# One table of step times for all engines in a stack of linear-attention layers, with eight shared PSUM banks

## The chip, the cores and the metric

The kernel runs on one core of a Trainium2 chip. The metric is device time in microseconds (us), from launch to finish, over repeated runs of the same program; less is better. A core has a matrix engine (TensorE, PE in the profile), which multiplies into PSUM, an on-chip memory of eight banks, and three engines that work on vectors: VectorE (DVE), ScalarE (ACT) and GpSimd (POOL). GpSimd has no part in reading PSUM in this kernel. DMA queues, most of them issued by the SyncE queue (SP), move data between device memory and the on-chip memory SBUF. Each engine works its own queue of instructions in order, and engines wait for each other by semaphores.

## What is computed

Two sequences of 2048 tokens with 256 features each, all in float32, go through two stacks. The first stack has three layers of causal linear attention (16 heads, 16 features each) with an MLP of 1024 hidden units:

```python
def favor(x, omega):
    xs = x * dh ** (-0.25)
    u = jnp.einsum('bshd,dm->bshm', xs, omega)
    h = 0.5 * jnp.sum(xs * xs, axis=-1, keepdims=True)
    return jnp.concatenate([jnp.exp(u - h), jnp.exp(-u - h)], axis=-1) * m ** (-0.5)

def step(carry, qkv):                      # causal linear attention, token by token
    Sst = Sst + ki[..., :, None] * vi[..., None, :]
    zst = zst + ki
    num = jnp.einsum('bhm,bhmd->bhd', qi, Sst)
    den = jnp.einsum('bhm,bhm->bh', qi, zst) + ATTN_EPS
    return ((Sst, zst), num / den[..., None])

for l in range(L):
    q, k, v = (out @ Wq[l] + bq[l]), (out @ Wk[l] + bk[l]), (out @ Wv[l] + bv[l])   # by heads
    a = causal_linear_attention(favor(q, omega[l]), favor(k, omega[l]), v) @ Wo[l] + bo[l]
    h = layer_norm(out + a, ln1_g[l], ln1_b[l])
    y = jax.nn.relu(h @ W1[l] + bf1[l]) @ W2[l] + bf2[l]
    out = layer_norm(h + y, ln2_g[l], ln2_b[l])
```

Its input is a normalized x, scaled and shifted by a conditioning vector; its output goes, gated, back onto x. The second stack has two layers of softmax attention in windows and a gated MLP. The change doesn't touch it.

## The kernel before

**Tiling.** The linear stack works on blocks of 256 tokens (TA): 2 sequences x 8 = 16 blocks, each through three layers, 48 layer passes in all. Between passes over the same sequence and layer, a running state (`state`, `zsum`) is carried, so a block's pass needs the state that the block before it left. A layer is `favor_layer` (L471). It has these steps, by the names of the tiles in the profile:

- projections `pq` (twice, queries and keys, L484) and `pv` (L500); VectorE adds the bias into `xs` (L495), ScalarE squares it (L496), VectorE fills `vp` (L511);
- features: `pu` (L525), eight matmuls that use 64 of the 128 columns of TensorE's array each (`tile_position=(0, 64 * hf)`), and their exponentials `ft` (L535); `qe` (L541), running sums `z` (L547, then GpSimd L556, L557), the transposed keys `tk` (L561) and `ktm` (L563);
- scores: `sc` (L572) for each half of 128 tokens, eight matmuls that use 32 of the 128 rows each, into four banks; VectorE masks each bank into `att` (L578);
- sums for the state: `su` (L592), `sum` (L600), `sth` and `st` on GpSimd (L612, L665); denominators `den` (L620) and `rb` (L622, L623);
- weighted values: `nd`, from the states with the whole array (L631), from the masked scores with 32 columns each (L644), then `aT` (L667);
- output projection `po` (L674), sum `s` (L682), the norm (`normed`: L422 to L430), its transpose `ntp` (L440), `h1` (L444);
- MLP: eight times `pf` (L696), `fr` (L704) and `acc` (L707), then the sum (L719), the norm, and the transpose into the next layer's `h`.

`scaled` (L453, L454, and L451 where a third operand is added) makes the residual on GpSimd. After the last layer a block's result is scaled onto its x, stored, normalized, transposed and stored again (`favor_block`, L763).

**Banks.** PSUM's eight banks are split in three: three for `mm_tile`, four shared by `sc` and `pf`, one for `acc`.

**Order.** `favor_layer` and `favor_block` are generators. Between two `yield`s lies a piece of TensorE work; the `yield` gives the planner `planned` (L91) a cost, a time until the next piece is due, a lock ("attention" or "mlp") and a piece of another block that must be done first. With at most four blocks in flight, the planner picks the piece that is due first. The order that results is fixed for TensorE alone (`manual_schedule(engines={PE})`, L793). The instructions of VectorE, ScalarE, GpSimd and the DMA queues are placed by the framework's own scheduler. It also picks the bank or buffer, out of those with the same tag, that a new tile gets.

The second stack already takes its steps from a table, `WHEN` (L124), on all four compute engines, with one pool of eight banks.

Of the kernel before, what the change touches and what calls it, by code (L numbers as in the profile page):

```python
# [39 lines left out]
def block_kernel(ctx: ExitStack, tc: tile.TileContext, t: dict, out: bass.AP):  # L40
# [48 lines left out]
    done = set()  # L89

    def planned(jobs, at_once):  # L91

        jobs, live, held, now, count = iter(jobs), [], {}, 0.0, 0
        while True:
            while len(live) < at_once:
                g = next(jobs, None)
                if g is None:  # L100
                    break
                live.append([now, count, g, None, None])
                count += 1
            if not live:
                return
            e = min(
                e[:2] + [e] for e in live
                if held.get(e[3], e) is e and (e[4] is None or e[4] in done)
            )[2]
            if e[3]:  # L110
                held[e[3]] = e
            step = next(e[2], None)
            keep = step[2] if step and len(step) > 2 else None
            for k in [k for k, o in held.items() if o is e and k != keep]:
                del held[k]
            if step is None:
                live.remove(e)
                continue
            now = max(now, e[0]) + step[0]
            e[0] = now + step[1]  # L120
            e[3:] = list(step[2:]) + [None] * (4 - len(step))
# [99 lines left out]
    with ExitStack() as c1:  # L221
        psum = c1.enter_context(tc.tile_pool(name="psA", bufs=1, space=PSUM))
        rp = c1.enter_context(tc.tile_pool(name="rA", bufs=2))
# [13 lines left out]

        def mm_tile(name):
            return psum.tile([P, TB], F32, tag="mm", name=name, bufs=3)
# [68 lines left out]
        def spread(lo, hi):  # L308
            n = (hi - lo) * KT
            tp = mm_tile("rowtp")[:n, :P]  # L310
            nc.tensor.transpose(tp, cols[:, lo:hi, :].rearrange("p a k -> p (a k)"), ident)
            turned_ = turned_cols.pop()[:n]
            nc.scalar.copy(turned_, tp)
            nc.gpsimd.dma_start(rows_out[lo * KT : hi * KT], turned_)
            nc.gpsimd.dma_start(
                brow[:, lo:hi, :].rearrange("p a d -> p (a d)"),
                rows_out[lo * KT : hi * KT].rearrange("a c -> (a c)").partition_broadcast(P),
            )
# [41 lines left out]
        def first_norm(normed, turned):  # L360

            with tc.manual_schedule(
# [6 lines left out]
                pm = mm_tile("pm")  # L369
# [22 lines left out]
        def rest_of_setup():  # L392
            yield 0.0, 8.0, "mlp"
            pm = psum.tile([P, NCA * D], F32, tag="acc", name="pm2", bufs=1)
            for i in range(2, 6):
                condition(i, i + 1, pm)
                yield 1.7, 0.0, "mlp"
            conditioned(2, 6, pm)
            for l in range(1, LA):
                omega_rows(l)  # L400
            for i in (2, 5):
# [10 lines left out]
            yield 0.0, 2.5  # L412
            spread(R_GE, NROW)
            load_weights(2, "Wq", "Wk", "Wv", "Wo", "W1", "W2")
            yield 0.2, 0.0

        def normed(src, dn=None):

            mv = work.tile([P, NCA, 2], F32, tag="mv", name="mv")
            for c in range(NCA):  # L420
                bs = work.tile([P, 6], F32, tag="bs", name="bs")
                nc.vector.bn_stats(bs, src[:, c, :])  # L422
                nc.vector.bn_aggr(mv[:, c, :], bs)
            rs = work.tile([P, NCA], F32, tag="rs", name="rs")
            nc.scalar.activation(rs, mv[:, :, 1], AF.Ln, bias=eps_t)
            nc.scalar.activation(rs, rs, AF.Exp, scale=-0.5)
            if dn is None:
                dn = work.tile([P, NCA, D], F32, tag="dn", name="dn", bufs=3)
            for c in range(NCA):
                nc.vector.tensor_scalar(  # L430
                    dn[:, c, :], src[:, c, :], mv[:, c, 0:1], rs[:, c : c + 1], ALU.subtract, ALU.mult
                )
            return dn

        def turned(dn, dst, gain, bias):

            tp = mm_tile("ntp").rearrange("p (k c) -> p k c", k=KT)
            for kt in range(KT):
                for c in range(NCA):
                    nc.tensor.transpose(  # L440
                        tp[:, kt, c * P : (c + 1) * P], dn[:, c, kt * P : (kt + 1) * P], ident
                    )
            for kt in range(KT):
                nc.scalar.activation(dst[:, kt, :], tp[:, kt, :], AF.Identity, bias=bias(kt), scale=gain(kt))  # L444

# [25 lines left out]
        def favor_layer(b, n, l, h, hres):  # L471
            va = V_A + l * VA_N

            def v(name, i=0):
                return vec[:, va + VA[name] + i : va + VA[name] + i + 1]

            xs = {}
            for wn, bn in (("Wq", "bq"), ("Wk", "bk")):  # L480
                pq = mm_tile("pq").rearrange("p (g c) -> p g c", g=KT)
                for g in range(KT):
                    for kt in range(KT):
                        nc.tensor.matmul(  # L484
                            pq[:, g, :],
                            W[wn, l][:, kt, g * P : (g + 1) * P],
                            h[:, kt, :],
# [3 lines left out]
                xs[wn] = fp.tile([P, 2, KT, TA], F32, tag="xs", name="xs", bufs=2)  # L491
                bias = vec[:, va + VA[bn] : va + VA[bn] + KT].unsqueeze(2).to_broadcast([P, KT, TA])
                for hf in range(2):
                    own, other = slice(64 * hf, 64 * hf + 64), slice(64 - 64 * hf, 128 - 64 * hf)
                    nc.vector.tensor_tensor(xs[wn][own, hf], pq[own], bias[own], ALU.add)  # L495
                    nc.scalar.activation(xs[wn][other, hf], xs[wn][own, hf], AF.Square)  # L496
            pv = mm_tile("pv").rearrange("p (c d) -> p c d", c=NCA)
            for c in range(NCA):
                for kt in range(KT):
                    nc.tensor.matmul(  # L500
                        pv[:, c, :],
                        h[:, kt, c * P : (c + 1) * P],
                        W["Wv", l][:, kt, :],
                        start=(kt == 0),
                        stop=(kt == KT - 1),
                    )

            vp = vpads[turn[0] % len(vpads)]
            turn[0] += 1
            for c in range(NCA):  # L510
                nc.vector.tensor_tensor(  # L511
                    vp[:, c, :, 0::3, :],
                    pv[:, c, :].rearrange("p (i q d) -> p i q d", q=2, d=16),
# [3 lines left out]
            yield 5.2, 0.6, "attention"  # L517
            if callable(hres):
                hres = hres()
            feat = []  # L520
            for wn in ("Wq", "Wk"):
                pu = mm_tile("pu").rearrange("p (g c) -> p g c", g=KT)
                for g in range(KT):
                    for hf in range(2):
                        nc.tensor.matmul(  # L525
                            pu[64 * hf : 64 * hf + 64, g, :],
                            omt[:, l, hf].rearrange("p h s m -> p (h s m)"),
                            xs[wn][:, hf, g, :],
                            start=True,
                            stop=True,  # L530
                            skip_group_check=True,
                            tile_position=(0, 64 * hf),
                        )
                ft = fp.tile([P, KT, TA], F32, tag=f"f{wn}", name="ft", bufs=1)
                nc.scalar.activation(ft, pu, AF.Exp)  # L535
                feat.append(ft)
            qf, kf = feat

            qe = sp.tile([P, KT, 2, TA], F32, tag="qe", name="qe", bufs=1)
            for q in range(2):  # L540
                nc.vector.tensor_scalar(qe[:, :, q, :], qf, par[:, q : q + 1], None, ALU.mult)  # L541
            yield 2.0, 1.0, "attention"

            z = fp.tile([P, KT, TA], F32, tag="z", name="z", bufs=1)
            zb = zsum.get((b, l))
            for g in range(KT):
                nc.vector.tensor_tensor_scan(  # L547
                    z[:, g, :],
                    kf[:, g, :],
# [5 lines left out]
            zsum[b, l] = sp.tile([P, KT], F32, tag=f"z{b}{l}", name="zl")  # L555
            nc.gpsimd.tensor_copy(zsum[b, l].unsqueeze(2), z[:, :, TA - 1 : TA])  # L556
            nc.gpsimd.tensor_tensor(z, qf, z, ALU.mult)  # L557
            tk = mm_tile("tk").rearrange("p (c g f) -> p c g f", c=NCA, g=KT)
            for c in range(NCA):
                for g in range(KT):  # L560
                    nc.tensor.transpose(tk[:, c, g, :], kf[:, g, c * P : (c + 1) * P], ident)  # L561
            ktm = fp.tile([P, NCA, KT, P], F32, tag="ktm", name="ktm", bufs=1)
            nc.scalar.copy(ktm, tk)  # L563

            def scores(c):

                cs = slice(c * P, (c + 1) * P)
                scs = [psum.tile([P, KT, 2, P], F32, tag="sc", name="sc", bufs=4) for _ in range(4)]
                for g in range(KT):
                    for i in range(4):  # L570
                        rs_ = slice(32 * i, 32 * i + 32)
                        nc.tensor.matmul(  # L572
                            scs[i][:, g], kf[rs_, g, cs], qe[rs_, g, :, cs], start=True, stop=True
                        )
                out_ = []
                for i in range(4):
# [948 lines left out]
```

## Time and profile before

| | us |
|---|---|
| median of 3 runs | 2959.73 |
| lowest, highest | 2957.91, 2963.54 |
| profiled execution | 2958.75 |
| its span, first to last instruction | 2957.0 |
| first projection of the linear stack (pq) starts | 11.63 |
| last MLP of the linear stack (acc) ends | 1560.36 |
| first projection of the second stack (pqkv) starts | 1561.36 |

| stretch, us | TensorE busy | VectorE busy | ScalarE busy | GpSimd busy |
|---|---|---|---|---|
| 0 to 60 | 48.92 | 38.61 | 20.06 | 28.57 |
| 120 to 1000 | 875.33 | 499.36 | 346.91 | 250.07 |
| 1000 to 1500 | 493.80 | 283.73 | 195.50 | 149.26 |
| 1700 to 1800 | 100.00 | 76.52 | 70.42 | 67.91 |

The page has one row for a group of instructions: line, engine, operation, the tiles written and read, their shapes, the count; then busy time in all and the mean of one in ns; then the idle time of the engine just before such instructions and what ended most of it. A row in order of time has the start, the duration (both in us), the engine, the line and the count. A TensorE row reads `128*32 128x256` where 128 rows and 32 columns of the array are used and 256 columns of data stream through. Each float32 matmul of the kernel is two records, a transpose is one.

### The profile page before, as it was taken

The page shows a single profiled execution, that of the slowest core. Times are in us where ns is not written, and L with a number is a line of the kernel's source. Part 1 is how long each engine was busy: PE and PEld are TensorE (multiplying, and loading weights), DVE is VectorE, ACT ScalarE, POOL GpSimd, SP SyncE. Part 2 cuts the span into 40 slices and gives each one's busy share as a digit, 9 for nine tenths or more (in the row PEclk, how much of TensorE's full clock was granted, in tenths as well). Part 3 has the DMA queues.
Part 4 walks back from the last instruction along what each step waited for, and adds up shares of the span by engine and source line. Part 5 has one row for each costly group of instructions (what it writes and reads, how often), then busy time and mean ns, then how long its engine had stood idle before and what let it go on. Part 6 is the DMA issues. An engine that isn't in the chain of part 4 may idle for free.

```text
span 2957.0 us, 49152 instructions
## 1 busy us (share of the span) xinstructions
PE 2904.0 (98%) x19323; PEld 2125.8 (72%) x19323; DVE 1688.3 (57%) x4186; ACT 1339.7 (45%) x3263; POOL 1068.9 (36%) x937
## 2 busy tenths in 40 slices
PE   8999999999999999999998999999999999999999
PEld 6888888888888888788875777775444777776444
DVE  6555556555655555655546777773224777774222
ACT  3343344343433343434335766675114667666211
POOL 4222233222332223322235666662002666663000
PEclk9999999999999999999999999999999999999999
DMA  6000010000100001001011000001000000000011
GB/s 218 1 1 1 5 39 15 1 1 1 41 18 1 1 1 37 19 1 44 16 54 39 5 20 1 1 1 58 0 0 10 1 20 1 1 1 8 29 43 36
DMA packets 38791, 58.96 MB, mean 20 GB/s; under 512 B 4702, under 2 KB 29856, under 8 KB 37920
## 3 DMA queue, kind: packets, MB, share of 16 engines
q1 hardware_dynamic: 36608, 51.33, 5.4%
q8 instruction: 153, 2.51, 0.4%
q0 software_dynamic: 1136, 3.44, 0.3%
q10 hardware_dynamic: 816, 1.05, 0.1%
q14 instruction: 78, 0.64, 0.1%
HBM read 43.73 MB, written 12.08 MB: 19 GB/s over the span
## 4 chain that ended last, share of the span: by engine, by line
PE 88%; DVE 5%; ACT 3%; POOL 2%; issue 1%; DMA 0%; SPq 0%; DVEq 0%; ACTq 0%; POOLq 0%
PE pf L696 11%; PE acc L707 11%; PE pqkv L914 9%; PE pg L1259 6%; PE pq L484 5%; PE acc L1297 5%; PE pa L1259 5%; PE av L1103 3%; PE ptp L1077 3%; PE sim L1010 3%; PE po L1122 3%; PE nd L644 3%; PE sc L572 3%; PE pu L525 3%; PE pv L500 3%; PE po L674 3%
## 5 line engine op out<-in xcount | busy, mean ns | idle before, releaser
L696 PE MATMUL pf<-h,wa 128*128 128x256 f32 x1536 | 402.5, 385 | 0.6 <-DVE att L578 0.3
L707 PE MATMUL acc<-wb,fr 128*128 128x256 f32 x1536 | 397.4, 382 | 4.8 <-ACT fr L704 4.4
L704 ACT ACTIVATE fr<-pf,vec 128x256 f32<-128x256 f32 x384 | 180.6, 471 | 429.4 <-PE pf L696 428.6
L914 PE MATMUL pqkv<-wqkv,s 128*128 128x512 f32 x768 | 352.0, 594 | 1.0 <-PE acc L707 1.0
L578 DVE TENSOR_TENSOR att<-sc,cst 128x512 f32<-128x512 f32 x384 | 238.1, 681 | 157.5 <-PE sc L572 157.5
L707 PEld LDWEIGHTS acc<-wb,fr 128*128 128x128 f32 x1536 | 288.5, 190 | 51.4 <-ACT fr L704 7.7
L696 PEld LDWEIGHTS pf<-h,wa 128*128 128x128 f32 x1536 | 277.3, 191 | 55.5 <-issue 19.8
L453 POOL TENSOR_TENSOR res<-dn,brow 128x512 f32<-128x512 f32 x110 | 143.4, 1304 | 457.6 <-DVE dn L430 442.0
L1065 POOL TENSOR_TENSOR pm<-pm,sum 128x1024 f32<-128x1024 f32 (+1 forms) x128 | 235.7, 1842 | 181.9 <-DVE sum L1060 181.9
L1050 ACT ACTIVATE pm<-pm,mx 128x256 f32<-128x256 f32 (+1 forms) x512 | 249.6, 488 | 60.3 <-DVE mx L1042 60.1
L956 POOL TENSOR_TENSOR rot<-raw,rsn_wo 128x512 f32<-128x512 f32 x128 | 160.7, 1276 | 197.9 <-ACT raw L937 194.7
L914 PEld LDWEIGHTS pqkv<-wqkv,s 128*128 128x128 f32 x768 | 136.3, 191 | 126.4 <-issue 124.0
L1268 DVE SCALAR_TENSOR_TENSOR ge<-pa,vec,ge 128x512 f32<-128x512 f32 x80 | 60.0, 751 | 280.7 <-PE pa L1259 229.4
L1267 ACT ACTIVATE ge<-pg,vec 128x512 f32<-128x512 f32 x96 | 65.8, 685 | 314.6 <-PE pg L1259 314.6
L496 ACT ACTIVATE xs<-xs 64x512 f32<-64x512 f32 x192 | 120.6, 628 | 152.9 <-DVE xs L495 143.6
L1259 PE MATMUL pg<-s,w 128*128 128x512 f32 (+1 forms) x384 | 182.2, 597 | 0.0
L484 PE MATMUL pq<-h,wa 128*128 128x256 f32 x768 | 177.4, 385 | 0.7 <-ACT h L444 0.7
L495 DVE TENSOR_TENSOR xs<-pq,vec 64x512 f32<-64x512 f32 x192 | 132.2, 688 | 75.8 <-PE pq L484 72.0
L1297 PE MATMUL acc<-ge,w 128*128 128x512 f32 (+1 forms) x384 | 168.8, 600 | 0.0
L484 PEld LDWEIGHTS pq<-h,wa 128*128 128x128 f32 x768 | 147.4, 193 | 22.9 <-issue 1.4
L1122 PEld LDWEIGHTS po<-oT,rsn_wo 128*128 128x128 f32 x1024 | 125.5, 194 | 38.1 <-issue 26.8
L978 POOL TENSOR_TENSOR qk<-qk,rot 128x1024 f32<-128x1024 f32 x64 | 151.3, 2365 | 0.5
(177 smaller groups left out, 5371.6 us busy)
## 6 DMA issues: line engine op xcount, KB each, us to landing
xin<-in_x_dram SPq DMA_DIRECT2D x30, 256.0 KB, 3.0
xl<-x SPq DMA_DIRECT2D x8, 512.0 KB, 4.3
out_dram<-res SPq DMA_DIRECT2D x8, 512.0 KB, 3.1
w<-in_w_dram SPq DMA_DIRECT2D x6, 640.0 KB, 4.1
x<-res SPq DMA_DIRECT2D x14, 256.0 KB, 2.1
h<-hm SPq DMA_DIRECT2D x14, 256.0 KB, 2.4
wa<-in_W_dram SPq DMA_DIRECT2D x3, 1024.0 KB, 11.1
wb<-in_W_dram SPq DMA_DIRECT2D x3, 1024.0 KB, 12.0
```

The costliest lines, as they stand in the source:

```text
L484: nc.tensor.matmul(pq[:, g, :], W[wn, l][:, kt, g * P : (g + 1) * P], h[:, kt, :], start=(kt == 0), stop=(kt == KT - 1),)
L578: nc.vector.tensor_tensor(am, scs[i].rearrange("p g q c -> p (g q) c"), caus.unsqueeze(1).to_broadcast([P, 2 * KT, P]), ALU.mult,)
L696: nc.tensor.matmul(pf, W["W1", l][:, kt, f * P : (f + 1) * P], h1[:, kt, :], start=(kt == 0), stop=(kt == KT - 1),)
L704: nc.scalar.activation(fr[f], pf, AF.Relu, bias=v("bf1", f))
L707: nc.tensor.matmul(acc[:, c, :], fr[f - 1][:, c * P : (c + 1) * P], W["W2", l][:, f - 1, :], start=(f == 1 and c == 0), stop=(f == NF), sk ...
L914: nc.tensor.matmul(pq, s[:, kt * TB + c * P : kt * TB + (c + 1) * P], wqkv[:, kt, i * INNER : (i + 1) * INNER], start=(kt == 0), stop=(kt ...
L956: nc.gpsimd.tensor_tensor(rot[:, :, :, lo : lo + 32], got["raw"][:, :, :, hi : hi + 32], rsn[:, ti, :, lo : lo + 32].unsqueeze(2).to_broad ...
L1050: nc.scalar.activation(pm[:, hd, :], pm[:, hd, :], AF.Exp, bias=of("mx", hg)[:, hd : hd + 1], accum_out=of("sum", hg)[:, hd : hd + 1],)
L1065: nc.gpsimd.tensor_tensor(pm, pm, of("sum", hg).unsqueeze(2).to_broadcast([P, 4, kw]), ALU.mult)
L1122: nc.tensor.matmul(po[:, m, :], wo[:, k, m * P : (m + 1) * P], got["oT"][:, k, :], start=(k == 0), stop=(k == INNER // P - 1),)
L1259: nc.tensor.matmul(pt[:m, :], w1[:, kt, off : off + m], hb[:, kt * TB : (kt + 1) * TB], start=(kt == 0), stop=(kt == KT - 1),)
L1297: nc.tensor.matmul(acc[m], w2[rs_, f, m * P : (m + 1) * P], g[rs_, :], start=(f == 0), stop=(f == NFH - 1),)
```

## The change

The generators and the planner go. `favor_layer(k)` now returns the steps of layer pass k as named functions, and a table gives each name a time, in units of one layer pass. Step `name` of pass k is placed at k + WHEN_A[name]; all steps are sorted by that, and TensorE, VectorE, ScalarE and GpSimd take them in this order (from 49.6 on only TensorE's is fixed). Passes go by fours: layer 0 of four blocks, layer 1 of the same four, layer 2, then the next four blocks. So passes k and k + 4 belong to the same block, or, after a third layer, to the block that leaves and the one that enters.

Besides this: all tiles in PSUM come from one pool of eight banks (`bank`); the features `pu` (step U) are cut into 16 matmuls of 32 columns instead of 8 of 64; the weighted values take both states first and then the scores of both halves; there are 10 instead of 8 buffers of masked scores, 2 instead of 1 of query features, 2 instead of 3 of `h1`; the loads for the second stack are issued two passes before the last.

```diff
-    def planned(jobs, at_once):
...
+    WHEN_A = {
+        "load": -1.9, "x0": -1.316, "x1": -1.297, "xr": -1.273, "xd0": -1.252, "xd1": -1.237,
+        "xput": -1.236, "T2": -1.23, "resB": -1.218, "h": -1.189, "Pq": -1.174, "Pk": -1.118, "xq0":
+        -1.085, "xq1": -1.063, "sq0": -1.057, "sq1": -1.035, "xk0": -1.029, "xk1": -1.007, "sk0":
+        -1.001, "sk1": -0.979, "U": -0.917, "fq": -0.849, "fk": -0.814, "qe0": -0.725, "qe1":
+        -0.705, "z0": -0.685, "z1": -0.659, "zl": -0.629, "zm": -0.622, "Pv": -0.455, "vp0": -0.372,
+        "vp1": -0.358, "K": -0.188, "ktm": -0.136, "S0": 0.0, "a0": 0.033, "a1": 0.055, "a2": 0.078,
+        "a3": 0.1, "S1": 0.139, "D": 0.167, "b0": 0.186, "b1": 0.208, "r0": 0.22, "M": 0.223, "b2":
+        0.23, "r1": 0.243, "b3": 0.252, "sum": 0.366, "half": 0.42, "N1": 0.938, "st": 0.999, "N2a":
+        1.028, "N2": 1.056, "aT": 1.122, "O": 1.307, "s0": 1.389, "s1": 1.403, "n0": 1.416, "n1":
+        1.435, "rs": 1.46, "dn0": 1.481, "dn1": 1.496, "resA": 1.515, "T1": 1.531, "h1": 1.572,
+        "f0": 1.629, "f1": 1.658, "r0_": 1.684, "g0": 1.686, "f2": 1.714, "g1": 1.742, "r1_": 1.742,
+        "r2_": 1.769, "f3": 1.784, "r3_": 1.848, "g2": 2.195, "f4": 2.251, "g3": 2.279, "r4_":
+        2.304, "f5": 2.363, "g4": 2.391, "r5_": 2.417, "f6": 2.419, "g5": 2.447, "f7": 2.475, "r6_":
+        2.476, "g6": 2.503, "r7_": 2.53, "g7": 2.601, "t0": 2.656, "t1": 2.67, "m0": 2.684, "m1":
+        2.703, "rt": 2.727, "e0": 2.748, "e1": 2.763, "put": 2.764, "x2": 2.79, "y0": 2.93, "y1":
+        2.95, "yr": 2.975, "yd0": 2.995, "yd1": 3.01, "T3": 3.215, "hm": 3.235,
+    }
+    RAMP = [
+        {"resB": 0.62},
...
+    SETUP_A = [-0.84, -0.15, 0.15, 0.16, 0.3, 0.5, 0.8]
+    TAIL_A = 49.6
...
+        def bank(name):
+            return psum.tile([P, TB], F32, tag="ps", name=name, bufs=8)
...
+        OPEN = 4
+
+        def favor_layer(k):
+
+            l = k % (OPEN * LA) // OPEN
+            b, n = blk = blocks[k // (OPEN * LA) * OPEN + k % OPEN]
...
+            @op("U")
+            def _():
+                for j in range(2):
+                    pu = got["pu", j] = both_halves(bank("pu"))
+                    for g in range(KT):
+                        for i in range(4):
+                            nc.tensor.matmul(
+                                pu[32 * i : 32 * i + 32, g, :],
+                                omt[:, l, i // 2, 2 * (i % 2) : 2 * (i % 2) + 2].rearrange(
+                                    "p h s m -> p (h s m)"
+                                ),
+                                got["xs", j][:, i // 2, g, :],
...
+                                tile_position=(0, 32 * i),
+                            )
...
+        steps = []
+        for k in range(len(blocks) * LA):
+            for name, f in favor_layer(k).items():
+                steps.append((k + WHEN_A[name] + (RAMP[k].get(name, 0.0) if k < len(RAMP) else 0.0), k, f))
+        setup = rest_of_setup()
+        steps += [(w, 0, partial(next, setup)) for w in SETUP_A]
+        steps.append((len(blocks) * LA - 2.0, 0, next_weights))
+        steps.append((len(blocks) * LA + 1.8, 0, lambda: scale_tables(*attn_w[0][1:4])))
+        steps.sort(key=lambda e: e[:2])
+        every = [getattr(mybir.EngineType, e) for e in ("PE", "DVE", "Activation", "Pool")]
+        with tc.issue_after(last_first):
+            for engines, lo, hi in ((every, -9.0, TAIL_A), (every[:1], TAIL_A, 99.0)):
+                with tc.manual_schedule(engines=set(engines)):
+                    for w, _, f in steps:
+                        if lo <= w < hi:
+                            f()
```

The step names, by the tiles they write: T2 and h (transpose and scale of the layer's input), resB (its residual, GpSimd), Pq, Pk, Pv (projections), xq, xk, sq, sk (`xs` and its squares), vp, U, fq, fk (features), qe, z, zl, zm, K and ktm (transposed keys), S0, S1 (scores of each half), a0 to a3 and b0 to b3 (their masks), D, r0, r1 (denominators), M, sum, half, st (state), N1 (`nd` from the states), N2a, N2 (from the scores), aT, O (`po`), s, n, rs, dn, T1, h1, resA (first norm), f0 to f7 (`pf`), r0_ to r7_ (`fr`), g0 to g7 (`acc`), t, m, rt, e (second norm); for a first layer load, x0 to xd1 (norm of x); for a third layer x2 (`scaled` onto x, three GpSimd operations, and a store), y0 to yd1, T3, hm (norm, transpose and store).

## The prediction

> **What bounds the kernel now.** I read the page from the top, then the chain, then TensorE's rows in order of time.
>
> ```profile
> span 2957.0 us, 49152 instructions
> PE 2904.0 (98%) x19323; PEld 2125.8 (72%) x19323; DVE 1688.3 (57%) x4186; ACT 1339.7 (45%) x3263; POOL 1068.9 (36%) x937
> ...
> PE 88%; DVE 5%; ACT 3%; POOL 2%; issue 1%; DMA 0%; SPq 0%; DVEq 0%; ACTq 0%; POOLq 0%
> ```
>
> TensorE is the bound; no other queue is near it, so a shorter TensorE queue shortens the run if its inputs stay on time. The change touches the linear stack alone, whose TensorE work runs from 11.63 us to 1560.36 us. TensorE's rows for parts of one layer there:
>
> ```profile
> 1007.14 3.62 PE L484 MATMUL pq<-h,wa 128*128 128x256 f32 x16
> ...
> 1013.63 1.03 PE L707 MATMUL acc<-wb,fr 128*128 128x256 f32 x4
> 1014.58 1.95 PE L525 MATMUL pu<-xs,omt 128*64 128x256 f32 x16
> 1016.46 1.13 PE L696 MATMUL pf<-h,wa 128*128 128x256 f32 x4
> 1017.43 1.03 PE L707 MATMUL acc<-wb,fr 128*128 128x256 f32 x4
> 1018.29 0.60 PE L561 MATMUL tk<-cst,ft 128*128 128x128 f32 x4
> 1018.82 1.15 PE L572 MATMUL sc<-qe,ft 32*128 32x256 f32 x16
> 1019.90 1.16 PE L592 MATMUL su<-vp,ktm 128*128 128x128 f32 x8
> ...
> 1028.65 0.61 PE L631 MATMUL nd<-ft,sth 128*128 128x128 f32 x4
> 1029.19 1.95 PE L644 MATMUL nd<-att,vp 128*32 128x128 f32 x64
> 1031.08 1.13 PE L707 MATMUL acc<-wb,fr 128*128 128x256 f32 x4
> ...
> 1038.53 3.62 PE L484 MATMUL pq<-h,wa 128*128 128x256 f32 x16
> ```
>
> Starts are what counts: ends are modelled and overlap. A layer takes 1038.53 - 1007.14 = **31.38 us**, without idle. A full-array record of 256 columns takes 0.216 us (four from one start to the next: 0.865), one of 128 columns 0.108. Where part of the array is used, records run side by side: 16 of pu two abreast should take 1.73, 16 of sc four abreast 0.865, 64 of nd 1.73. From 1013.63 to 1017.43 are 3.80 us for 0.865 + 1.73 + 0.865 = 3.46: 0.34 is lost around the features. In the same way 0.44 is lost around the first scores (tk to the pf at 1020.89), 0.41 around the second, 0.37 around the weighted values (1028.65 to 1032.05). Some **1.55 us** a layer is lost by changing the array's form; 29.84 is work.
>
> **Part 1: the forms stand together.** Sorted by the fraction of their step times, TensorE's steps are S0, N2a, N2, U, S1, then full-array work: one visit to the divided array per layer, not four. U is recut from 64 to 32 columns, so it shares N2's form. A visit's loss, taken apart at the rows: about 0.10 in the full group before it, 0.21 after a row-divided group, 0.16 after a column-divided one, 0.10 in the full group that follows. Does a change from one divided form straight into another cost more? The second stage has one:
>
> ```profile
> 1601.42 1.04 PE L1077 MATMUL ptp<-cst,pm 128*128 128x128 f32 x8
> 1602.39 2.00 PE L1010 MATMUL sim<-kT,qT 64*128 64x256 f32 x16
> 1604.32 1.97 PE L1103 MATMUL av<-pT,v 128*64 128x128 f32 x32
> 1606.21 0.49 PE L1145 MATMUL var<-both,cst 128*128 128x128 f32 x2
> 1606.54 1.88 PE L914 MATMUL pqkv<-wqkv,s 128*128 128x512 f32 x4
> ```
>
> 5.12 us for 0.87 + 1.73 + 1.73 + 0.22 = 4.55: 0.57, the sum of the same terms (0.10 + 0.20 + 0.16 + 0.11). So the new visit costs 0.10 + 0.21 + 0.16 + 0.21 + 0.10 = 0.78, the layer 29.84 + 0.78 = **30.62**, and 48 layers save 48 x 0.76 = **36.5 us**. Ends: 0 (a change between divided forms costs like two) to 48 x 1.55 = 74; the second stage's row decides.
>
> U now has 16 matmuls of 32 columns instead of 8 of 64. nd L644 has just that form: 64 records in 1.73 us is fully four abreast, so U stays at 1.73. [...] The 768 weight loads more lie beside matmuls: nd's 64 already do.
>
> **Part 2: all queues by the table.** The planner cost nothing at run time. What is new is that VectorE, ScalarE and GpSimd take their steps in the table's order. I laid the order out: each queue in order, each step starting when its inputs are there, lasting what its row lasts.
>
> ```profile
> L578 DVE TENSOR_TENSOR att<-sc,cst 128x512 f32<-128x512 f32 x384 | 238.1, 681 | 157.5 <-PE sc L572 157.5
> L453 POOL TENSOR_TENSOR res<-dn,brow 128x512 f32<-128x512 f32 x110 | 143.4, 1304 | 457.6 <-DVE dn L430 442.0
> L495 DVE TENSOR_TENSOR xs<-pq,vec 64x512 f32<-64x512 f32 x192 | 132.2, 688 | 75.8 <-PE pq L484 72.0
> ```
>
> A consumer starts 0.20 us after the matmul group it reads. In an ordinary layer nothing is late: nearest are Pq behind h, g0 behind its relu (0.865 of f1 covers 0.20 + 0.47 + 0.05) and T2 behind e1 (0.8 spare). The eight banks just suffice: S1 needs four while sums, nd and two pu hold the rest, so it starts only after mask a3, done about 3.7 us after S0's start; S1 is due at 4.7.
>
> **At a change of blocks it is late.** Blocks go in fours, and while one finishes (x2: three GpSimd operations) the next enters (x0 to xd1, resB). GpSimd has resB (0.782) ahead of x2 (0.790): five operations, 4 x 1.36 (start to start) + 1.28 = 6.7 us after xd1. xd1 ends some 6.2 us before S0 (T2, f3, K, Pq, Pk, N1 lie between), so x2 ends 0.6 after S0. VectorE has y0, which needs x2, ahead of xq1: then y0 0.56, xq1 0.70, y1 0.56, xk0 and xk1 0.70 each, yd0 and yd1 0.35 each, 3.9 in all, and only then the masks: a0 at 4.6, a3 done at 7.1. U waits behind sk1, S1 behind a3: together 2.6 us instead of 0. Both norms before T2 add 0.8 at g1 and T2 (ScalarE has rt and xr ahead of r1_). The first and last layer of such a group carry one part each: 38.8 us for the three changes together. Without this collision that part would be 0; with every VectorE, ScalarE and GpSimd duration 5% longer it and the ramp come to 12 more.
>
> **The ramp.** Early layers have little to put between. T2 of layer 2 stands behind a VectorE order of sum(0), vp(1), x0(2) and waits 7.4 us, T2 of layer 3 2.8, Pq 0.9: 11.1. The first 16 pq records took 6.74 instead of 3.46 us (granted clock 0.91 over the first 60 us, 1.00 after); that stays, 3.3. [...] The tail adds 0.5.
>
> **Moves at the end.** Stage two's four attention loads go out some 1.5 layers earlier; the setup's late loads keep their order. SP is not in the table and DMA is busy 6%, so I cost them at nothing; landing late, they would hold the second stage's first projection, 4 to 12 us by the landing rows. More buffers of masks and query features hide waits and add none. scale_tables stays after the last layer.
>
> **The sum.** Before: 48 x 31.38 + 14 x 0.43 (third transposes) + 4.1 (conditioning and row transposes) = 1516.3, against 1560.4 - 11.6 = 1548.7: 32.4 lost to ramp, slow clock and tail. After: 48 x 30.62 + 10.1 = 1479.9, lost 38.8 + 11.1 + 6.7 + 0.5 = 57.1, ending at 11.6 + 1479.9 + 57.1 = 1548.6. So -36.5 + 24.7 = **-11.8 us**. The rest follows TensorE's end as before (first pqkv 1.0 us after it). The profiled execution took 2958.75 us, 1.75 more than its span, and lies 1.0 under the median of 2959.73: 2959.7 - 11.8 = **2948 us**. 0.2% (5.9 us) is about what a measurement of this kernel can tell from no change.
>
> **Rivals.**
> (a) The block changes cost little, because GpSimd or VectorE has slack that I don't see: some 30 of the 38.8 us stay in hand, **2918**. For it: GpSimd is idle 64%. Against: the order of five operations is fixed.
> (b) Slower: a bank wait on every layer takes the place of the switches. All eight banks are in one pool and S1, K or N1 may be handed one that frees late; if the most recently freed bank is always handed out, my layout gives 32.1 us a layer and 84 us more in all. It decides from 0.25 us a layer (48 x 0.25 = 12). For it: spare at S1 is 1 us, and four-bank groups leave no choice. Against: the second stage uses such a pool, and from 1700 to 1800 us its TensorE is busy 100.00 of 100 us. At 0.75 a layer: -12 + 36 = **2984**.
> [...]
>
> **Numbers.** My forecast 0.52, (a) 0.18, (b) 0.22, (c) 0.08. Of the forecast's own spread (2936 to 2962) about 0.38 lies below -0.2%, 0.09 within, 0.05 above. Faster 0.38 + 0.18 = 0.56, same 0.09, slower 0.05 + 0.22 + 0.08 = 0.35. The range leaves the best of (a) and the worst of (b) out: 2912 to 2988; the forecast's own is 2936 to 2962.
>
> **What the changed profile would show.** TensorE rows sc, nd, nd, pu (128*32, x32), sc back to back; first-score starts 30.6 us apart in ordinary layers, about 34 in the four layers of each block change, with waits for att and xs there, and y0's statistics waiting for GpSimd's res. [...] Wrong altogether: the second stage starting later after stage one's end than 1 us.

## The result and the profile after

The changed kernel takes **2950.19 us** (median of six runs, 2946.49 to 2952.51); six runs of the kernel before on the same chip have a median of 2961.23 (2957.91 to 2963.54). The ratio is 0.9963, 95% interval 0.995 to 0.9976: 11 us faster. The forecast was 2948 us, 11.8 less than before. The profiled execution took 2947.69 us, 1.79 more than its span.

The top of the page of the kernel after, and the end of its chain:

```profile
span 2945.9 us, 50382 instructions
PE 2891.0 (98%) x20091; PEld 2136.8 (73%) x20091; DVE 1676.9 (57%) x4186; ACT 1344.7 (46%) x3263; POOL 1059.9 (36%) x937
...
PE 90%; DVE 4%; ACT 2%; POOL 1%; issue 1%; DMA 1%; SPq 0%; DVEq 0%; ACTq 0%; POOLq 0%
```

TensorE is still the bound. The second stack's first projection starts at 1550.48 us instead of 1561.36, and from there to the span's end it is 1395.4 us against 1395.6 before: in these two executions all of the gain lies in the linear stack.

**The gain: one visit a layer.** TensorE's rows of the kernel after, in order of time (start, duration in us), around the scores of an ordinary layer:

```profile
1053.24 0.61 PE L793 MATMUL nd<-ft,sth 128*128 128x128 f32 x4
1053.78 1.15 PE L708 MATMUL sc<-qe,ft 32*128 32x256 f32 x16
1054.85 1.95 PE L808 MATMUL nd<-att,vp 128*32 128x128 f32 x64
1056.62 1.91 PE L636 MATMUL pu<-xs,omt 128*32 128x256 f32 x32
1058.46 1.15 PE L708 MATMUL sc<-qe,ft 32*128 32x256 f32 x16
1059.54 1.13 PE L773 MATMUL den<-z,cst 128*128 128x256 f32 x4
1060.51 1.03 PE L889 MATMUL acc<-wb,fr 128*128 128x256 f32 x4
```

Scores, weighted values, features and scores of three layers stand together. Take the starts and subtract the work (0.43, 0.865, 1.73, 1.73, 0.865, 0.865): 0.11 is lost before the scores, 0.21 after them, 0.04 + 0.11 from nd over pu to the second scores, 0.21 after these, 0.10 in the denominators: 0.78, as forecast. The features' 32 records take the 1.73 us of four abreast and the loss of the change after them. First scores of ordinary layers start 30.65 us apart (108.37 to 139.02), against 31.38 before; four early ones, which have no carried state to multiply yet, take 30.20.

**Where it is given back: a change of blocks.** First scores there start at 352.51, 386.79, 421.08 and 455.36: 34.28 us apart (33.97 at the other two changes). The same rows in one such layer:

```profile
378.13 1.03 PE L870 MATMUL pf<-h,wa 128*128 128x256 f32 x4
379.61 1.13 PE L889 MATMUL acc<-wb,fr 128*128 128x256 f32 x4 [0.46 <-ACT fr L881]
380.58 0.64 PE L465 MATMUL ntp<-cst,dn 128*128 128x128 f32 x4
...
386.79 1.15 PE L708 MATMUL sc<-qe,ft 32*128 32x256 f32 x16
387.87 1.96 PE L808 MATMUL nd<-att,vp 128*32 128x128 f32 x64
389.64 2.73 PE L636 MATMUL pu<-xs,omt 128*32 128x256 f32 x32
392.30 2.76 PE L708 MATMUL sc<-qe,ft 32*128 32x256 f32 x16
395.00 1.13 PE L773 MATMUL den<-z,cst 128*128 128x256 f32 x4
```

From pu to den are 5.36 us, in the ordinary layer 2.92: 2.44 lost, though no row shows idle time. The waits lie between the records inside a group, so that its duration grows (2.73 and 2.76 instead of 1.91 and 1.15); one who adds up the waits of TensorE's rows misses them. At acc and ntp another 0.72 goes (1.48 from the start of pf to that of acc and 0.97 from acc to ntp, instead of 0.865 each), and the third transposes are 0.43 of work: 3.59 of the 3.63 us. What VectorE waits for, in GpSimd's rows and then in VectorE's, same layer of the kernel after:

```profile
380.69 1.27 POOL L485 TENSOR_TENSOR res<-dn,brow 128x512 f32<-128x512 f32 x1 [7.30 <-DVE dn L444]
382.04 1.27 POOL L486 TENSOR_TENSOR res<-res,brow 128x512 f32<-128x512 f32 x1
383.26 1.27 POOL L483 TENSOR_TENSOR xin<-xin,brow 128x512 f32<-128x512 f32 x1
384.48 1.27 POOL L485 TENSOR_TENSOR res<-dn,brow 128x512 f32<-128x512 f32 x1
385.84 1.26 POOL L486 TENSOR_TENSOR res<-res,xin 128x512 f32<-128x512 f32 x1
```

```profile
387.13 0.43 DVE L431 BATCH_NORM_STATS2 bs<-res 128x6 f32<-128x256 f32 x1 [2.17 <-POOL res L486]
...
391.40 2.48 DVE L720 TENSOR_TENSOR att<-sc,cst 128x512 f32<-128x512 f32 x4
```

Five operations of GpSimd, the two of resB first; x2 ends at 387.10, 0.31 after the first scores' start; y0's statistics wait for it, and the masks start at 391.40, 4.61 after the first scores. Over the three changes the intervals exceed 30.65 by 14.6 + 13.3 + 13.2 = 41.1 us, of which 12 x 0.43 = 5.2 is the transposes' work: 35.9 us of waits.

**Ramp and tail.** TensorE's rows of the kernel after, once near the start and once near the end of the linear stack:

```profile
44.80 1.13 PE L465 MATMUL ntp<-cst,dn 128*128 128x128 f32 x4 [7.76 <-DVE dn L444]
45.73 0.42 PE L317 MATMUL rowtp<-cst,stage 128*8 128x128 f32 x1
45.94 1.06 PE L691 MATMUL tk<-cst,ft 128*128 128x128 f32 x4
46.95 5.12 PE L577 MATMUL pq<-h,wa 128*128 128x256 f32 x16
51.91 0.61 PE L793 MATMUL nd<-ft,sum 128*128 128x128 f32 x4
...
1472.47 2.58 PE L708 MATMUL sc<-qe,ft 32*128 32x256 f32 x12 [1.66 <-DVE att L720]
1474.98 2.07 PE L773 MATMUL den<-z,cst 128*128 128x256 f32 x4
1476.85 1.91 PE L889 MATMUL acc<-wb,fr 128*128 128x256 f32 x4
1478.56 1.75 PE L733 MATMUL su<-vp,ktm 128*128 128x128 f32 x8
1480.15 1.03 PE L870 MATMUL pf<-h,wa 128*128 128x256 f32 x4
```

In the ramp, the norm's transposes of layer pass 2 wait 7.76 us. The granted TensorE clock is 0.50 from 39.59 to 49.83 us, so the work behind the wait runs slower (16 projections in 4.96 instead of 3.46): 7.11 us for 0.43 + 0.11 + 0.44 + 3.46 = 4.44, so 2.7 are lost. In the tail the second scores of pass 46 wait 1.66 us for a mask, and the next four groups take nearly double: acc 1.71 to the next start instead of 0.865. Why the mask is late, VectorE's rows show:

```profile
1466.58 1.29 DVE L720 TENSOR_TENSOR att<-sc,cst 128x512 f32<-128x512 f32 x2 [0.54 <-PE sc L708]
1469.52 2.29 DVE L191 TENSOR_TENSOR rc_qks<-rc_qks 128x2048 f32<-128x2048 f32 x1 [1.65 <-DMA rc_qks<-in_k_scale_dram]
1471.73 1.28 DVE L720 TENSOR_TENSOR att<-sc,cst 128x512 f32<-128x512 f32 x2
```

Between the second and the third mask VectorE multiplies a table of the second stack (`scale_tables`), after 1.65 us of waiting for a load into it. So the third mask starts 3.86 us after the second one's end. In the change's list this step stands at 49.8, behind TAIL_A = 49.6, where only TensorE's order is fixed; on VectorE it runs among the masks of pass 46. It does so in the kernel after and in all eleven experiments; none of them moves it.

### The profile page after: what moved, and what is told of

Its sections match the earlier page's. It is cut to its first block, busy times and chain, and to the rows that moved or that the text cites. A ratio compares the mean times of both kernels' runs of the same rounds, so it can differ in the third digit from the quotient of the medians.

```text
span 2945.9 us, 50382 instructions
## 1 busy us (share of the span) xinstructions
PE 2891.0 (98%) x20091; PEld 2136.8 (73%) x20091; DVE 1676.9 (57%) x4186; ACT 1344.7 (46%) x3263; POOL 1059.9 (36%) x937
## 4 chain that ended last, share of the span: by engine, by line
PE 90%; DVE 4%; ACT 2%; POOL 1%; issue 1%; DMA 1%; SPq 0%; DVEq 0%; ACTq 0%; POOLq 0%
PE acc L889 11%; PE pf L870 10%; PE pqkv L1091 9%; PE pq L577 6%; PE pg L1436 6%; PE acc L1474 5%; PE pa L1436 5%; PE sc L708 4%; PE av L1280 3%; PE ptp L1254 3%; PE sim L1187 3%; PE po L1299 3%; PE pu L636 3%; PE nd L808 3%; PE pv L609 3%; PE po L828 3%
## 5 line engine op out<-in xcount | busy, mean ns | idle before, releaser
L870 PE MATMUL pf<-h,wa 128*128 128x256 f32 x1536 | 386.7, 379 | 0.0
L870 PEld LDWEIGHTS pf<-h,wa 128*128 128x128 f32 x1536 | 284.5, 190 | 35.4 <-ACT h L473 0.7
L680 POOL COPY zl<-z 128x2 f32<-128x2 f32 x48 | 9.0, 187 | 507.2 <-DVE z L668 507.2
## 6 DMA issues: line engine op xcount, KB each, us to landing
wa<-in_W_dram SPq DMA_DIRECT2D x3, 1024.0 KB, 11.1
```

Source lines behind the costliest of these rows:

```text
L870: nc.tensor.matmul(pf, W["W1", l][:, kt, f * P : (f + 1) * P], got["h1"][:, kt, :], start=(kt == 0), stop=(kt == KT - 1),)
```

## The experiments

Each changes the kernel after, mostly times in its table; none leaves work out. Ratios are to the kernel before on the same chip.

**1. Later norms.** VectorE's steps of the leaving block's norm are put behind the masks.

```diff
-"y0": 2.93, "y1": 2.95, "yr": 2.975, "yd0": 2.995, "yd1": 3.01, "T3": 3.215, "hm": 3.235
+"y0": 3.53, "y1": 3.55, "yr": 3.575, "yd0": 3.6, "yd1": 3.615, "T3": 3.765, "hm": 3.785
```

> The steps y0 to hm of a leaving block are placed 0.55 to 0.6 of a layer later; nothing else changes. Theory (the block changes are slow because VectorE's fixed order has y0, which waits for five GpSimd operations, ahead of xq1, xk and the masks): the 2.6 us a layer at U and S1 go, the 0.8 us at g1 and T2 stay: some 29 us less than the changed kernel, about 2921 us, first-score starts at block changes 31.5 us apart instead of 34.3. Rival (the wait only passes on, or VectorE's load in these layers is what is too long): 2945 to 2952 us.

Measured: 2928.03 us, ratio 0.9891 (0.9874 to 0.9907), 22 us under the kernel after, where some 29 were expected. The layers at a change of blocks take 32.11 instead of 34.28; 31.5 was expected.

**2. GpSimd takes x2 first.** One number.

```diff
-"resB": -1.218
+"resB": -1.205
```

> Only GpSimd's order changes: resB behind x2 (0.795 instead of 0.782). Theory (the wait for GpSimd's five operations is the cause, not VectorE's load): x2 ends 2.1 us before S0 instead of 0.6 after, y0 is on time, and the gain is the same 29 us, about 2921 us. Rival (VectorE simply has too much to do between Pk and the masks at a block change): half of it or less, 2935 us or more.

Measured: 2922.79 us, ratio 0.9873 (0.9859 to 0.9888), 27 us under the kernel after. The layers take 32.02. Its rows in the layer that was shown above, GpSimd's, TensorE's, VectorE's:

```profile
380.53 1.27 POOL L486 TENSOR_TENSOR res<-res,xin 128x512 f32<-128x512 f32 x1
```

```profile
385.50 1.15 PE L708 MATMUL sc<-qe,ft 32*128 32x256 f32 x16
...
388.35 1.91 PE L636 MATMUL pu<-xs,omt 128*32 128x256 f32 x32
...
391.45 1.13 PE L773 MATMUL den<-z,cst 128*128 128x256 f32 x4
```

```profile
387.85 2.49 DVE L720 TENSOR_TENSOR att<-sc,cst 128x512 f32<-128x512 f32 x4
```

x2 ends at 381.80, 3.70 ahead of the first scores. VectorE does the same work in the same order, but its masks start 2.35 and not 4.61 us after the first scores, and pu to den is 3.10 us, 0.18 over an ordinary layer. So it was GpSimd's order that set the wait, not the amount of VectorE's work: with the latter, this edit would have changed nothing. The intervals at the changes exceed 30.65 by 16.3 us in all instead of 41.1: 24.8 us. The tail's interval, from the last first scores but one to the last, is 29.77 instead of 33.00, which is no merit of the edit (see the end); the ramp is 1.3 us longer and the start 0.3 earlier: the second stack starts 27.1 earlier. It then takes 1397.4 us, 2.0 more than in the kernel after, though the edit doesn't touch it (see the end).

**3 and 4. Divided visits again.** A full-array group of the MLP is put between nd and pu, and in the second kernel another between pu and the second scores.

```diff
-"g2": 2.195, "g3": 2.279
+"g2": 2.07,  "g3": 2.279        (one split)
+"g2": 2.07,  "g3": 2.12         (two splits)
```

> One full-array MLP group (g2) is placed between the weighted values and the features, so the divided array is visited twice a layer instead of once; the work is the same. Theory (each further visit costs 0.16 + 0.10 + 0.10 = 0.36 us): 48 x 0.36 = 17 us more, about 2967 us, ordinary layers 31.0 us. Rival (the gain of the change came from the new order of the queues, not from the array's form): 2948 to 2953 us.

> As the run before, and another full-array group (g3) between the features and the second scores: three visits a layer. Theory: 48 x 0.72 = 35 us more than the changed kernel, about 2985 us, ordinary layers 31.35 us; that is the time of the planner's four visits but one, and so slower than the kernel before, because the block changes are not covered any more. Rival: 2948 to 2956 us.

Measured: 2946.69 us, ratio 0.9951 (0.9936 to 0.9966), and 2944.3, 0.9944 (0.9929 to 0.9959). The kernel after has 0.9963 (0.995 to 0.9976): the intervals overlap, and neither kernel is 17 or 35 us slower. Yet ordinary layers did become longer, by 0.335 us (30.98) and 0.53 (31.18). The layer at a change of blocks shows the rest, TensorE's rows of the kernel with one split:

```profile
392.14 1.13 PE L889 MATMUL acc<-wb,fr 128*128 128x256 f32 x4
393.20 1.93 PE L636 MATMUL pu<-xs,omt 128*32 128x256 f32 x32
```

acc has moved into the time in which the features and second scores were waiting: the layer takes 33.42 instead of 34.28, with two splits 32.56. With one split the last first scores start at 1494.89 us instead of 1498.42. Between: 29 ordinary layers +9.7, the three changes -9.3, the tail's interval (28.84 for 33.00) -4.2, ramp and start +0.3: -3.5. Of the tail's 4.2, 3.3 are the slow clock of the kernel after, of which this execution shows nothing: den there takes 0.97 us to the next start, not 1.87 (see the end); without it cost and gain of the split are even. These two can't price a split, because the collision covers it. My expectation had another fault too: the second split parts pu from the scores, which differ in form anyway, so it adds one change, not two.

**5 and 6. The same without the collision:** x2 first, and the splits.

```diff
-"resB": -1.218, "g2": 2.195, "g3": 2.279
+"resB": -1.205, "g2": 2.07,  "g3": 2.279        (one split)
+"resB": -1.205, "g2": 2.07,  "g3": 2.12         (two splits)
```

> The kernel of e2 (no collision at the block changes) with g2 between the weighted values and the features. Theory A (a form change costs time in every layer; in e3 this was there, and was paid back at the block changes, where the inserted group covers part of the wait for the masks): e3's ordinary layers were 0.34 us longer, so 48 x 0.34 = 16 us over e2, 2939 us. Rival B (a form change costs nothing to the whole; what TensorE loses there it would lose elsewhere): 2923 us, as e2.

> The kernel of e2 with both groups inserted as in e4. The second one parts two different forms, so it adds one change and not two: e4's ordinary layers were 0.53 us longer than those of the changed kernel. Theory A: 48 x 0.53 = 26 us over e2, 2948 us. Rival B: 2923 us.

Measured: 2932.38 us, ratio 0.9908 (0.9893 to 0.9922), and 2943.05, 0.994 (0.9925 to 0.9955): 9.6 and 20.3 us over the kernel with x2 first alone, where 16 and 26 were expected (the two pairs ran on different chips, on which the kernel before differs by 0.9 us). TensorE's rows with one split, in an ordinary layer:

```profile
1047.46 1.96 PE L808 MATMUL nd<-att,vp 128*32 128x128 f32 x64
1049.35 1.13 PE L889 MATMUL acc<-wb,fr 128*128 128x256 f32 x4
1050.41 1.93 PE L636 MATMUL pu<-xs,omt 128*32 128x256 f32 x32
1052.28 1.15 PE L708 MATMUL sc<-qe,ft 32*128 32x256 f32 x16
```

0.16 after nd, 0.20 in acc, 0.14 after pu, against 0.04 and 0.11 with the forms together: 0.35, and every ordinary layer takes 30.98. At a change of blocks the period rises by 0.16 only (32.18 after 32.02), and the tail's interval falls by 0.95: there the group still covers a wait. So 29 ordinary layers pay 9.7, the changes 2.8, the tail -0.95, and the first scores came 0.3 earlier: the second stack starts 11.2 us later. The price per layer was right; that all 48 would pay it was not. With two splits it is 0.53 a layer, 0.36 at a change. That is 0.53 of the 0.73 us that the change saves; no run parts the first scores from the weighted values again.

**7. Features at 64 columns.** x2 first, and U as before the change, in 8 matmuls.

```diff
-    for i in range(4):    ... pu[32 * i : 32 * i + 32, g, :] ... tile_position=(0, 32 * i)
+    for hf in range(2):   ... pu[64 * hf : 64 * hf + 64, g, :] ... tile_position=(0, 64 * hf)
```

> The kernel of e2 with the features cut into 8 matmuls of 64 columns as before the change, in the same place. Theory: 64 columns are a third form, one more change (some 0.2 us) a layer, while the features themselves take the same 1.73 us: 48 x 0.2 = 9 us over e2, 2932 us. [...]

Measured: 2928.22 us, ratio 0.9895 (0.9879 to 0.9912), 5.4 over x2 first alone, where 9 were expected; in the profiled execution 3.3 of it are lost in the tail, where groups take up to twice their time (see the end). From nd to the second scores are 3.76 us and not 3.61: 64 columns after 32 is one form more. An ordinary layer takes 30.80 instead of 30.65. So four abreast lost nothing against two abreast, and the recut is worth 0.15 a layer.

**8. An earlier norm in the ramp.** x2 first, and layer pass 2's entering norm 0.35 of a pass sooner.

```diff
 RAMP[2]:
-{}
+dict.fromkeys(("load", "x0", "x1", "xr", "xd0", "xd1", "xput"), -0.35)
```

> The kernel of e2 with the first norm of layer pass 2 (load to xput) placed 0.35 earlier, ahead of sum(0) and vp(1) in VectorE's order. Theory: the wait of 7.8 us at T2 of pass 2 goes, and with it the slow TensorE clock behind it (pq 4.96 instead of 3.46 us, T2 and tk 1.0 more): 8 to 10 us less than e2, 2914 us. Rival (the wait moves to N1 of pass 0, which needs sum and half, and the clock stays): 2920 to 2923 us.

Measured: 2926.24 us, ratio 0.9881 (0.9867 to 0.9896): no gain. TensorE's rows:

```profile
40.81 1.14 PE L465 MATMUL ntp<-cst,dn 128*128 128x128 f32 x4 [3.54 <-DVE dn L444]
45.47 0.37 PE L317 MATMUL rowtp<-cst,stage 128*8 128x128 f32 x1 [3.52 <-DVE stage L308]
```

The first wait is halved, and a row transpose of the setup, whose place in the queue is ahead of the second pass's keys, takes over the other half. It waits for VectorE's setup steps; tk starts at 45.64 in this kernel and in the one with x2 first alone. The second stack starts 0.3 us later than there (1523.69) and takes 3.3 more, untouched by the edit: this, and no cost of the edit, is what lifts the profiled time above x2 first.

**9 to 11. That row moved, and a relu.** x2 first once more; with the ramp's edit and the setup's last part later; and with r1_ also ahead of xr on ScalarE.

```diff
-SETUP_A = [-0.84, -0.15, 0.15, 0.16, 0.3, 0.5, 0.8]
+SETUP_A = [-0.84, -0.15, 0.15, 0.16, 0.3, 0.5, 1.25]     (10 and 11)
-"r1_": 1.742
+"r1_": 1.726                                             (11)
```

> The kernel with x2 before resB once more, so that the two beside it are compared on the same chip: 2921 to 2926 us, as before. TensorE waits for the transposed norm of layer 2 in the ramp for 7.8 us and twelve times 0.46 us for the relu ahead of its second group.

> Layer 2's norm is entered earlier, as in the kernel that moved the wait from 7.76 us to 3.54 + 3.52 us, and the last part of the setup (the row transpose that waited 3.52 us for a staged row) is put behind the second layer's values instead of ahead of its keys. Theory that the ramp's wait was only held by that row: the 3.5 us go, keys of the second layer start at about 42.1 us and not 45.6, so the time is some 3.5 us under the kernel with x2 first, 2919 to 2921; and if the shorter idle stretch no longer slows the clock, the 16 query projections take 3.46 and not 5.0 us and it is 5 us under. Rival, that VectorE's own work is what the ramp waits for: the wait moves on to the next step that needs VectorE (the sum of keys and values, or the masks), first scores of the second layer stay at 52.2 us, and the time is that of the kernel beside it.

> As the one before, and ScalarE applies the relu ahead of the second group of the feed-forward product before the next layer's residual row (r1_ at 1.726, ahead of xr at 1.727). Theory: the twelve waits of 0.46 us go, one in each layer of a change of blocks, 5.5 us less than the kernel beside it, so 2914 to 2917 if that one gains 3.5 us. Rival: xr and with it the third transposes come later by the length of the relu, 0.47 us, and the wait moves from the product to the transposes: no gain.

Measured: 2922.02 us (2921.61 to 2925.48), ratio 0.9873 (0.9858 to 0.9888); 2919.85 (2917.18 to 2922.35), 0.9863 (0.9848 to 0.9878); **2918.2** (2916.62 to 2920.7), 0.9858 (0.9842 to 0.9875). The ramp of the second, TensorE's rows:

```profile
40.44 1.14 PE L465 MATMUL ntp<-cst,dn 128*128 128x128 f32 x4 [3.54 <-DVE dn L444]
...
42.23 5.56 PE L577 MATMUL pq<-h,wa 128*128 128x256 f32 x16
47.62 0.61 PE L793 MATMUL nd<-ft,sum 128*128 128x128 f32 x4
```

The wait of 3.52 us is gone, the row transpose no longer stands here, and the first scores of pass 1 start at 48.16 us, not at 52.24 as in experiment 8 or at 50.94 as in the kernel with x2 first beside it: the theory of the held row is right. Its second half is not. The 16 projections take 5.39 us where that kernel, after a wait of 7.75, has 4.29: behind the wait of 3.54 us the mean clock is 0.61 over 7.16 us (40.44 to 47.60), and that takes back 1.1 of the gain. The second stack starts 2.6 us earlier (1519.83 after 1522.47); the medians differ by 2.2, and their ranges overlap; in the profiled execution the second stack then takes 3.4 us more, which is more than the gain. For the relu the rival had the larger part: the twelve waits of acc (5.5 us) are gone, but the transposes now wait for VectorE's dn (16 waits, 10.2 us, after 4 of 6.3). At the first change of blocks the period stays 32.02, at the other two it falls from 31.99 to 31.70: 8 x 0.29 = 2.3 us, beside medians 1.7 apart with overlapping ranges.

## Why the prediction was right, point by point

The linear stack ended 0.8 us after the time that the sum gave (1549.4 for 1548.6). It also began 0.6 earlier, so the sum itself is 1.4 us short. Its terms, as the prediction put them, against the rows:

| term, us | predicted | measured | difference |
|---|---|---|---|
| an ordinary layer | 30.62 | 30.65 | +1.4 in 48 |
| six passes without a carried state | not counted | 0.44 less each | -2.6 |
| waits at the three changes of blocks | 38.8 | 35.9 | -2.9 |
| waits in the ramp | 11.1 | 10.8 (7.76 + 2.3 + 0.7) | -0.3 |
| slow first projections | 3.3 | 2.5 | -0.8 |
| slow clock after T2 of pass 2 | 3.4 | 2.7 | -0.7 |
| tail | 0.5 | 6.2 | +5.7 |

These differences come to -0.2, so 1.6 us are not placed.

- **Forms together**: held to 0.03 us a layer, with the loss in the places named. Experiments 5 and 6 show it from the other side: each full group put between costs 0.2 to 0.34 in every ordinary layer.
- **U at 32 columns**: nd's row, which has the same form, held: the features' 32 records take 1.84 us to the next start (1056.62 to 1058.46), 1.73 of work and 0.11 of change. The forecast had the price of recutting right; that the recut itself gains, 0.15 a layer, experiment 7 shows.
- **Change of blocks**: the order of five GpSimd operations, x2's end after the first scores (0.31 us, forecast 0.6), the first mask 4.61 after them (4.6) and the last one's end 7.1 after (7.1) all came. The delay at U and S1 is 2.44 (2.6), at g1 and T2 0.72 (0.8). Experiment 2 shows the cause: of the 35.9 us, 24.8 hang on which of two operations GpSimd takes first. Of the 11.1 that stay, 5.5 are the twelve waits of acc for a relu, of which experiment 11 removes 2.3 and moves the rest.
- **Slow clock after the ramp's wait**: no run shows the 3.4 us that the sum's 6.7 has for it beside the 3.3 of the first projections; measured are 2.7, and 2.0, 2.3 and 2.8 in experiments 9, 2 and 10. In the kernel before, den took 1.87 us to the next start after a wait of 2.06, where a later one takes 0.97 (60.53 to 61.50), a loss of 0.9:

```profile
31.74 2.08 PE L620 MATMUL den<-z,cst 128*128 128x256 f32 x4 [2.06 <-POOL z L557]
33.61 1.71 PE L324 MATMUL pm<-stage,wmod 128*128 128x2 f32 x8
```

The price didn't end with that group. Over it and what came behind it the clock stayed at half for 6.5 us of TensorE work (the third number from the end is the clock), which is a loss of 3.3:

```profile
31.43:38.26 6.83, 6.52 (x48) 0.50 0.82 260
```

- **First projections**: they were slow again, but the profile's clock reads 1.00 over them, before and after (its records begin at 17.78 and 15.70 us). The prediction's 0.91 over the first 60 us comes from two later stretches (31.43 to 38.26 and 55.33 to 58.74). What slows the first projections is not shown.
- **Moves at the end**: what follows the linear stack takes 1395.4 us against 1395.6, as costed. But scale_tables, which the prediction keeps after the last layer, ran on VectorE among the masks of pass 46, and the prediction has no term for that.
- **The tail is the step that was mis-sized.** I allowed 0.5 for it. The second scores lose 2.9 us to masks that stand behind scale_tables: 2.1 before the last twelve and 0.8 among them (at full clock, in experiment 2, these take 1.66 to the next start, for 0.65 of work and 0.21 of change). The slow clock that follows takes another 3.3. With the group that experiment 5 puts ahead of the features, the wait falls from 1.74 to 0.45. That the total was close is in part luck: the other terms together were 5.9 us too dear.

Of the rivals, (a) was right that GpSimd had room and wrong that the order as written would use it: it forecast 2918 us, and experiments 2, 9 and 11 (the last with edits to ramp and relu besides) come to 2922.8, 2922.0 and 2918.2. (b), a bank wait in every layer, is not seen: ordinary layers are alike, and work and visit (29.84 + 0.78) leave 0.03 of their 30.65. (c) in the chances, a visit that saves less than forecast, is out by its rows, which lose the 0.78 of the forecast.

## What to carry to other kernels

An order fixed by a table has to be checked at the seams (a block leaving while another enters, the ramp, the tail), since a queue of an engine that is idle 64% of the time, GpSimd's, held the bound one: here the order of two steps was worth 24.8 us, more than twice the whole net gain. Where an order is fixed for one engine alone, look at where the other engines run the steps behind it: here a later stage's step came to stand between two masks. Price an edit in the layers that have no slack and count those that do apart; an edit tried on top of a collision (experiments 3 and 4) measures the collision. Where a group of matmuls is longer than its like elsewhere, look at start-to-start times, because the waits inside a group (here 5.36 us from pu to den for 2.92) showed in no column of idle time.

## What was not expected of the hardware

**The same wait was followed by different clocks.** In eight of the profiles the tail's wait is 1.65 to 1.78 us long. It stands at the same place in the order. Stretches of the kernel after and then of the one with x2 first; behind the comma stands TensorE's busy time, and the third number from the end is its granted clock:

```profile
1469.78:1473.19 3.41, 1.75 (x18) 1.00 0.16 42
1473.19:1480.02 6.83, 6.83 (x25) 0.50 0.01 2
```

```profile
1444.74:1448.15 3.41, 2.21 (x36) 1.00 0.41 150
1448.15:1451.56 3.41, 2.88 (x18) 1.00 0.00 0
```

The same four groups (from the twelve second scores to the end of su) take 4.38 us in experiments 2, 9 and 1, 6.06, 6.06 and 6.02 in 8, 10 and 11, 7.36 in 7, where the next group takes 1.19 instead of 0.865 besides, and 7.68 in the kernel after. So 0, 1.7 or 3.3 us are lost. In the kernel after that is half of the 6.83 us at clock 0.50; in experiment 8 it is half of 3.4 us, which is what its mean clock of 0.72 over 6.07 us (1447.33 to 1453.40) comes to; in experiment 2, which loses nothing, the clock is 1.00 (1448.70 to 1453.00).

In the profiles of the kernels before and after, the stretches at half clock begin at 31.43, 55.33, 1485.51, 1591.33 and 2953.24 us, and at 39.59, 1473.19, 1582.41 and 2940.92: within each profile a whole number of steps of 3.413 us apart. All but the one at the run's end last one, two or three such steps. In the kernel after all 1.66 us of the tail's wait lie in one step (1469.78 to 1473.19), and the clock fell at its end; in experiment 2, 1.20 us of the wait lie in the first of the two stretches above and the rest in the second, and it did not fall. From 20 us to the stretch at the run's end, the clock of these two kernels fell behind seven steps, which have 1.66 to 3.41 us of TensorE idle time each, and behind none with less; but behind one with 1.68 it stayed full (kernel after, 1568.76 to 1572.17 us). What decided there stays open, as does how many steps the half clock lasts.

So the 27.1 us by which the second stack starts earlier with x2 first hold 3.3 that are the clock's. The second stack itself, the same in every run, takes from 1395.3 us (experiment 1) to 1400.8 (experiment 6); the mean clock of the whole execution is 0.995 in 4, 6, 8 and 10, which need about 1400 us for it, 0.996 in 11, which needs 1399.5, and 0.996 or 0.997 in the others, which need 1395.3 to 1397.4. Differences of a few us between two kernels here say little.

**The longer wait had no higher price.** In the ramp, a wait of 3.54 us (experiment 10) was followed by 2.8 us of loss, one of 7.76 (kernel after) by 2.7 and one of 7.75 (experiment 9) by 2.0, reckoned alike from the first row behind the wait to the end of the 16 projections. In the kernel after the half clock began during the wait, at 39.59 us, and 5.03 us of it lay behind the wait, half of which is 2.5; in experiment 10 the mean clock of 0.61 over the 7.16 us behind the wait comes to 5.6 us at half, half of which is 2.8. Halving the wait here saved the wait, not the slow stretch behind it.
